# Silu on ScalarE in place of tanh and a VectorE product in one layer of a four-layer graph kernel, and table loads in its instruction planner

## The chip, the cores and the metric

The kernel runs on one core of a Trainium2 chip. Five engines of the core matter here. TensorE (PE in the profile) does matrix products and transposes into the eight banks of PSUM. VectorE (DVE) and ScalarE (ACT) do elementwise work; ScalarE also evaluates functions such as Tanh, Exp, Ln and Silu, which it reads from a table that a separate instruction loads. GpSimd (POOL) does a few small powers and one addition per group. SyncE (SP) issues most transfers. Each engine works through its own queue in order, and engines wait for each other by semaphores.

The metric is device time in microseconds (us) of one execution, as the median of several runs. All data are float32.

## What is computed

The input is 128 graphs with 64 nodes and 256 features, a 0/1 adjacency matrix for each and a node mask. Four layers follow each other; each adds its result to its input and normalizes the rows.

```
def _L0_gnn_ref(...):                      # gated graph layer, 5 steps
    A = (adj != 0).astype(x.dtype)
    for l in range(5):
        m = jnp.einsum('bnd,de->bne', h, weight[l])
        agg = jnp.einsum('bij,bid->bjd', A, m)
        h = _gru_cell(agg, h, w_ih, w_hh, b_ih, b_hh)   # 2 sigmoids, 1 tanh
    return h * mask[..., None]

def _L1_gnn_ref(...):
    agg = epsilon * x + einsum('bnm,bmd->bnd', adjacency, x)
    h = einsum('bnd,dh->bnh', agg, W1) + b1             # 256 -> 1024
    h = jax.nn.silu(h * rsqrt(mean(h*h) + eps) * rms_weight)
    return einsum('bnh,hd->bnd', h, W2) + b2            # 1024 -> 256

# layer 2: artanh of the row norm, product with adj, tanh of the row norm, projection
# layer 3: attention with exp(e_i + f_j), masked by adj

x = _layernorm(x + _L0_gnn_ref(...)); x = _layernorm(x + _L1_gnn_ref(...))
x = _layernorm(x + _L2_gnn_ref(...)); x = _layernorm(x + _L3_gnn_ref(...))
```

## The kernel before, in words

**Tiling.** Eight graphs form a group: four blocks of 128 rows, two graphs in each block. There are 16 groups (0 to 15). `group(g)` records all four layers of a group. Layer 0 (`gated`, called five times) works on features by rows (`hT`), in two halves of 256 rows; its products are `p_r`, `p_in`, `p_hn`, `p_u`, `p_v`, `p_w` (L663), its tanh instructions stand at L767 and L780, and its new state `hT` is formed by three VectorE instructions at L782, L786 and L788. `ps_hr` (L643) are transposes of the state, `ps_agg` (L333) products with the adjacency.

**The order of the work is planned.** Nothing is issued while `group` runs. Each call of `flow.op` records an operation with its engine, a cost in us written by hand (`act`, `dve`, `pe`, `pool` give it from the width), and what it reads and writes; `flow.either` records one that ScalarE or VectorE may take (`copied` L349 and L350, `scaled` L354 and L355). At the end `flow.issue` runs a beam search: `Plan.advance` picks, again and again, the operation that can start first by these costs, out of up to four groups at once (`WINDOW`) and within a look-ahead on each engine (`AHEAD`). The plan found is written into the program as the order of every engine's queue. So a change of a cost, or of one operation, can move any instruction of the program, and which of ScalarE and VectorE takes an `either`.

**Tables.** Before this change the planner knows nothing of table loads. The Ln of layer 2 (L975) is written down as if it were 2600 elements wide, which makes its cost 2.27 us, and the first Tanh (L466) costs 1.5 us. The loads themselves are put in when the program is built, ahead of an activation whose function is not in the table at hand. Tanh (L767, L780, L1012) and Exp (L1045) share one table, Ln needs another.

**Layer 1 of a group**, the place of the change:
- The rows after the first normalization (`x_n`) are multiplied with the adjacency into `ps_agg` and copied to `aggm`. POOL adds the bias b2 to `x_n` in one instruction of 128x1024 (`xb`, L853).
- The hidden layer has 1024 features in eight chunks of 128x512 (`hid`). Groups 0 to 13 form it with seven products in place of eight (`by_sums`, matmuls at L882, differences `t` at L878, sums at L887); groups 14 and 15, the last two, form it plainly (`as_it_is`, `ps_hid`, one copy per chunk).
- For each chunk ScalarE squares it (L868) and VectorE adds the squares (`sqs`, L870). TensorE sums over the features (`ps_ss`), VectorE scales (`ms`, L931), POOL takes the power -1/2 (`rms`, L933), TensorE spreads the result over the partitions (`ps_rms`, L936).
- For each chunk: VectorE adds the bias and multiplies with `ps_rms` (L941); ScalarE takes Tanh of it with the scale `half_r`, half the RMS weight (L944), into a buffer `th`; VectorE forms (th + 1) times the chunk (L946). With v the normalized chunk and w the RMS weight, this is 2 v sigmoid(w v).
- TensorE multiplies with W2 (`ps_o`, 32 calls of `matmul`, which the trace shows as 64 matmuls). The RMS weight that belongs in front of v was multiplied into W2 once, at the start (`w2s`, L590, eight instructions on ScalarE). VectorE takes half of the product and adds `xb` (L959).

Behind it stand the second normalization (statistics L673 and L674, `ve` L676, POOL's power L678, L680, `off` L684, `x_n` L354 or L355), layer 2 (`fac` with Ln at L975, `tan`, `ps_sup`, a row norm at L1006 and L1010, tanh at L1012, `y` at L1028) and layer 3 (`ps_T`, `ps_a`, Exp at L1045, `ps_att`, `y` at L1061).

## Time and profile before

| | |
|---|---|
| Five runs, us | 2431.09, 2433.07, 2432.07, 2430.45, 2430.65; median 2431.09 |
| The profiled execution, us | 2431.09 |
| Span of its profile, us | 2429.3 |
| Granted TensorE clock, mean | 0.996 |
| Read from and written to HBM, MB | 25.74 and 8.39 |

The profile is of one execution. Its span runs from the first instruction to the last one; the execution's own time is 1.8 us longer. PE is TensorE's matmuls, PEld its weight loads, which overlap them. Matmuls are pipelined, so one matmul of 128x256 is shown with about 379 ns while the next starts 216 ns after it; a busy TensorE may still hide short gaps. Idle time of an engine that is not the bottleneck costs nothing.

### The profile page before, as it was taken

How to read it: one execution, taken by the hardware profiler on the slowest of the kernel's cores; microseconds unless marked ns; L12 is line 12 of the kernel's file. 1: busy time of each engine (PE TensorE's matmuls, PEld its weight loads, DVE VectorE, ACT ScalarE, POOL GpSimd, SP SyncE). 2: the span in 40 equal slices, each digit the busy share in tenths (PEclk: the TensorE clock that was granted, in tenths of full speed). 3: DMA queues.
4: the chain of work that ended last, by engine and by line, in shares of the span. 5: the costliest groups of instructions: out<-in, count | busy, mean ns of one | idle time of the engine just before them, and what ended most of it. 6: DMA issues, size and time to landing. Idle time of an engine off the chain costs nothing.

```text
span 2429.3 us, 32703 instructions
## 1 busy us (share of the span) xinstructions
PE 2392.2 (98%) x12258; PEld 2101.7 (87%) x12258; DVE 1893.6 (78%) x4097; ACT 1148.3 (47%) x2408; POOL 188.4 (8%) x144
## 2 busy tenths in 40 slices
PE   9999999999999999999999999999999999999995
PEld 7888888888888888888888888888888888888864
DVE  3668787887888877778777887888787787878777
ACT  4434544454445444454444545455444544445453
POOL 4000000000100000000000100000000000000011
PEclk9999999999999999999999999999999999999998
DMA  4000000000000000000000000000000000000000
GB/s 126 4 1 12 1 29 1 18 12 1 29 1 27 3 18 11 1 27 3 11 19 1 29 1 27 3 18 11 1 29 1 18 12 1 27 9 18 9 9 18
DMA packets 39725, 36.21 MB, mean 15 GB/s; under 512 B 9956, under 2 KB 38656, under 8 KB 39568
## 3 DMA queue, kind: packets, MB, share of 16 engines
q1 hardware_dynamic: 37840, 32.25, 4.3%
q8 instruction: 97, 1.59, 0.3%
q10 hardware_dynamic: 1328, 1.31, 0.2%
q0 software_dynamic: 400, 0.57, 0.1%
q14 instruction: 60, 0.49, 0.1%
HBM read 25.74 MB, written 8.39 MB: 14 GB/s over the span
## 4 chain that ended last, share of the span: by engine, by line
PE 94%; DVE 4%; ACT 1%; DMA 1%; issue 0%; POOL 0%; SPq 0%; POOLq 0%; ACTq 0%; DVEq 0%
PE p_v L663 11%; PE p_w L663 11%; PE p_in L663 11%; PE p_r L663 11%; PE p_hn L663 11%; PE ps_o L333 9%; PE ps_agg L333 6%; PE p_u L663 6%; PE ps_hr L643 3%; PE ps_a L333 2%; PE p_wh L882 2%; PE p_vh L882 2%; PE p_1h L882 2%; PE ps_T L633 1%; PE ps_att L333 1%; PE p_uh L882 1%
## 5 line engine op out<-in xcount | busy, mean ns | idle before, releaser
L663 PE MATMUL p_hn<-hT,w_hn 128*128 128x256 f32 x1280 | 322.8, 380 | 0.0
L663 PE MATMUL p_in<-agg,w_in 128*128 128x256 f32 x1280 | 315.3, 379 | 0.0
L663 PEld LDWEIGHTS p_in<-agg,w_in 128*128 128x128 f32 x1280 | 240.2, 190 | 31.1
L663 PEld LDWEIGHTS p_hn<-hT,w_hn 128*128 128x128 f32 x1280 | 227.9, 191 | 22.7
L333 PE MATMUL ps_o<-w2s,hid 128*128 128x256 f32 x1024 | 231.2, 379 | 0.0
L333 PEld LDWEIGHTS ps_o<-w2s,hid 128*128 128x128 f32 x1024 | 193.9, 190 | 27.3 <-issue 1.2
L678 POOL TENSOR_TENSOR rstd<-ve,pow 128x4 f32<-128x4 f32 (+1 forms) x64 | 82.7, 1292 | 1492.0 <-DVE ve L676 1484.1
L767 ACT ACTIVATE V<-V,half_b 128x256 f32<-128x256 f32 x160 | 72.7, 500 | 199.2 <-DVE V L763 199.0
L663 PE MATMUL p_u<-tA,s 128*128 128x256 f32 x640 | 158.1, 381 | 1.4 <-DVE tA L746 0.6
L663 PE MATMUL p_w<-tA,s 128*128 128x256 f32 x640 | 158.1, 379 | 0.0
L663 PE MATMUL p_r<-hT,a 128*128 128x256 f32 x640 | 156.9, 379 | 0.0
L663 PE MATMUL p_r<-agg,a 128*128 128x256 f32 x640 | 156.7, 379 | 0.0
L663 PE MATMUL p_v<-tB,s 128*128 128x256 f32 x640 | 155.4, 379 | 0.0
L663 PE MATMUL p_v<-tB,na 128*128 128x256 f32 x640 | 154.5, 379 | 0.0
L663 PE MATMUL p_w<-hT,s 128*128 128x256 f32 x640 | 154.3, 379 | 0.0
L349 ACT COPY agg<-ps_agg 128x512 f32<-128x512 f32 x154 | 90.0, 585 | 114.0 <-PE ps_agg L333 98.5
L333 PEld LDWEIGHTS ps_agg<-edge,hr 128*128 128x128 f32 x1024 | 136.1, 191 | 6.6
L354 ACT ACTIVATE hnb<-p_hn,half_b 128x256 f32<-128x256 f32 x232 | 101.8, 473 | 81.3 <-PE p_hn L663 67.3
L333 PE MATMUL ps_agg<-edge,hr 128*128 128x128 f32 x1024 | 138.8, 275 | 0.0
L663 PEld LDWEIGHTS p_u<-tA,s 128*128 128x128 f32 x640 | 119.3, 190 | 21.0 <-DVE tA L746 2.3
L663 PEld LDWEIGHTS p_v<-tB,s 128*128 128x128 f32 x640 | 120.9, 190 | 16.3 <-PE ps_att L333 0.2
L663 PEld LDWEIGHTS p_w<-hT,s 128*128 128x128 f32 x640 | 120.7, 190 | 16.0
(233 smaller groups left out, 4682.5 us busy)
## 6 DMA issues: line engine op xcount, KB each, us to landing
x<-in_x_dram SPq DMA_DIRECT2D x16, 512.0 KB, 3.6
xr<-in_x_dram SPq DMA_DIRECT2D x16, 512.0 KB, 3.6
out_dram<-x_n SPq DMA_DIRECT2D x16, 512.0 KB, 2.9
edge<-in_adj_dram SPq DMA_DIRECT2D x32, 64.0 KB, 2.3
wm<-in_L_gnn_weight_dram SPq DMA_DIRECT2D x5, 256.0 KB, 5.3
w2s<-in_L_gnn_W_dram SPq DMA_DIRECT2D x1, 1024.0 KB, 10.2
w<-in_L_gnn_W_dram SPq DMA_DIRECT2D x2, 512.0 KB, 3.5
w_in_L_gnn_w_hh_dram<-in_L_gnn_w_hh_dram ACTq DMA_DIRECT2D x1, 512.0 KB, 5.2
```

Of the source, the lines that this page charges most:

```text
L333: return nc.tensor.matmul(o, lhsT, rhs, start=(k == 0), stop=(k == nk - 1))
L349: flow.either([("ACT", 0.27 + 0.00077 * n, lambda: nc.scalar.copy(o(), i())), ("DVE", 0.16 + 0.00105 * n, lambda: nc.vector.tensor_copy(o( ...
L354: flow.either([("ACT", 0.27 + 0.00077 * n, lambda: nc.scalar.activation(o(), i(), AF.Identity, bias=bias(), scale=scale())), ("DVE", 0.16 ...
L633: turn(lambda j=j, c=c: nc.tensor.transpose(ps[:, c * HR + j * P:c * HR + (j + 1) * P], src[:, 2 * n + j, c * P:(c + 1) * P], ident.tile() ...
L643: turn(lambda j=j, c=c: nc.tensor.transpose(ps[:, j * D + c * P:j * D + (c + 1) * P], src[:, c, (2 * n + j) * P:(2 * n + j + 1) * P], iden ...
L663: pe(256, lambda c=c, k=k: nc.tensor.matmul(ps[:, c * HR:(c + 1) * HR], w[:, k, c * P:(c + 1) * P], v(k), start=first and c == k == 0, sto ...
L678: pool(1.1, lambda: nc.gpsimd.tensor_tensor(rstd[:, :m, :], ve[:, :m, :], pow2[:, :m, :], OP.pow), [rstd], [ve])
L767: act(256, lambda c=c: nc.scalar.activation(o[:, c, :], src(c), AF.Tanh, bias=half_b[:, i * KD + c:i * KD + c + 1], scale=0.5), [(o, c)], ...
L882: pe(256, lambda c=c: nc.tensor.matmul(ps[:, c * HR:(c + 1) * HR], w1f[:, w, (2 * q + c) * P:(2 * q + c + 1) * P], v[0](), start=first and ...
```

## The change

Layer 1's activation becomes one ScalarE instruction per chunk, Silu in place, with the RMS weight as its scale per partition. The VectorE product L946 and the buffer `th` go, and with them the factors that belonged to them: `half_r`, the eight scalings of W2 and the factor 0.5 behind `ps_o`, which becomes a plain add.

```
-            th = u("VZR"[c % 3], f"th{c}")
-            act(512, lambda v=v, th=th, c=c: nc.scalar.activation(th.tile(), v, AF.Tanh, scale=half_r[:, c:c + 1]),
-                [th], [*parts, half_r])
-            dve(512, lambda v=v, th=th: nc.vector.scalar_tensor_tensor(
-                v, th.tile(), 1.0, v, OP.add, OP.mult), parts, [*parts, th])
+            act(512, lambda v=v, c=c: nc.scalar.activation(v, v, AF.Silu, scale=rmsc(c)), parts, [*parts, cols], SILU)
...
-                dve(256, lambda ps=ps, b=b, j=j: nc.vector.scalar_tensor_tensor(
-                    y1[:, b, :], ps[:, j * D:(j + 1) * D], 0.5, xb[:, b, :], OP.mult, OP.add), [(y1, b)], [ps, (xb, b)])
+                dve(256, lambda ps=ps, b=b, j=j: nc.vector.tensor_add(
+                    y1[:, b, :], ps[:, j * D:(j + 1) * D], xb[:, b, :]), [(y1, b)], [ps, (xb, b)])
...
-    dve(4, lambda: nc.vector.tensor_scalar(half_r.tile(), cols[:, 2 * NV + KH:], 0.5, None, OP.mult), [half_r], [cols])
...
-    for k in range(KH):
-        act(256, lambda k=k: nc.scalar.activation(w2s[:, k, :], w2s[:, k, :], AF.Identity, scale=rmsc(k)), [(w2s, k)], [(w2s, k), cols])
```

The planner learns of tables. An activation may carry `sets`, the tables that hold its function, the first being the one that a load would bring. A plan remembers the table at hand; an activation that is not in it is taken to start `TABLE` later. The costs that stood in for loads are taken back: in the planner's account Tanh is in the table of Exp and in that of Silu, Ln is 4 elements wide, and the first Tanh costs 0.2 us.

```
+    TABLE = 1.28
...
                             elif o.kb and e != "POOL":
                                 t = max(t, self.lands[0])
+                        elif o.sets and self.table not in o.sets:
+                            t += flow.TABLE
...
             _, o, eng, t = best
+            if o.sets and self.table not in o.sets:
+                self.table = o.sets[0]
...
+    TANH, EXP, LN, SILU = ("exp", "silu"), ("exp",), ("ln",), ("silu",)
...
-    def act(n, run, w, r):
-        flow.op("ACT", 0.27 + 0.00077 * n, run, w, r)
+    def act(n, run, w, r, sets=None):
+        flow.op("ACT", 0.27 + 0.00077 * n, run, w, r, sets=sets)
...
-    flow.op("ACT", 1.5, lambda: nc.scalar.activation(warm, one4, AF.Tanh))
+    flow.op("ACT", 0.2, lambda: nc.scalar.activation(warm, one4, AF.Tanh), sets=TANH)
...
-        act(2600, lambda: nc.scalar.activation(fac.tile(), fac.tile(), AF.Ln), [fac], [fac])
+        act(4, lambda: nc.scalar.activation(fac.tile(), fac.tile(), AF.Ln), [fac], [fac], LN)
```

The Tanh and Exp instructions of layers 0, 2 and 3 get their `sets` in the same way. Nothing else is computed differently.

## The prediction

> **What bounds the kernel now.** I read four views in this order: the page, a table of stretches, the waits of TensorE, the groups of instructions. The page first.

> ```profile
> span 2429.3 us, 32703 instructions
> ...
> PE 2392.2 (98%) x12258; PEld 2101.7 (87%) x12258; DVE 1893.6 (78%) x4097; ACT 1148.3 (47%) x2408; POOL 188.4 (8%) x144
> ```

> TensorE is busy for all but 37.1 us. The change touches none of its 12258 matmuls, so what it can win is in those 37.1 us, and what it can lose is new idle time there. So the question is where they lie. The table of stretches has one row per stretch: its length, then busy time and instruction count of PE, PEld, DVE, ACT and POOL, then the clock.

> ```profile
> 0.00:40.00 40.00, 36.12 (x181) 27.41 (x182) 16.03 (x45) 14.27 (x33) 9.02 (x16) 1.00 0.56 169
> 40.00:2300.00 2260.00, 2257.12 (x11665) 2000.88 (x11664) 1777.97 (x3775) 1071.11 (x2251) 160.67 (x116) 1.00 0.04 12
> 2300.00:2340.00 40.00, 36.03 (x156) 25.27 (x156) 31.41 (x55) 20.23 (x38) 6.61 (x4) 1.00 0.05 14
> 2340.00:2382.30 42.30, 42.30 (x181) 31.85 (x179) 32.62 (x72) 22.57 (x35) 3.66 (x3) 1.00 0.00 1
> 2382.30:2429.30 47.00, 20.63 (x82) 16.25 (x80) 35.53 (x150) 20.10 (x53) 8.40 (x7) 0.78 0.07 23
> ```

> Idle: 3.9 us in the start, 2.9 us in the 2260 us of the middle, 4.0 us where the last group enters layer 1 (2300 to 2340), none up to the last `ps_o` matmul at 2382.3, and 26.4 us in the 47.0 us behind it, a serial chain of the last two groups. The waits of TensorE in the middle, and then in 2300 to 2340 (who waited for whom: total, times, longest):

> ```profile
> PE p_uh L882 <- DVE t L878: 1.4, 4, 0.6
> PE p_u L663 <- DVE tA L746: 0.6, 1, 0.6
> PE p_u L663 <- ACT junk_a L1006: 0.5, 1, 0.5
> ```

> ```profile
> PE ps_hid L333 <- DVE aggm L350: 2.5, 1, 2.5
> PE ps_hr L643 <- DVE hT L788: 1.4, 1, 1.4
> ```

> VectorE stands behind most of it, ScalarE behind 0.5 us. The groups that the change removes or resembles (line, engine, operation, names, count | busy, mean ns | idle before):

> ```profile
> L944 ACT ACTIVATE th<-hid,half_r 128x512 f32<-128x512 f32 x128 | 88.0, 721 | 47.1 <-DVE hid L941 47.1
> L946 DVE SCALAR_TENSOR_TENSOR hid<-th,hid 128x512 f32<-128x512 f32 x128 | 82.7, 686 | 0.3 <-ACT th L944 0.2
> L959 DVE SCALAR_TENSOR_TENSOR xb<-ps_o,xb 128x256 f32<-128x256 f32 x64 | 24.4, 420 | 55.1 <-PE ps_o L333 55.1
> L975 ACT ACT_TABLE_LOAD x15 | 19.2, 1283 | 0.3
> L767 ACT ACT_TABLE_LOAD x10 | 12.8, 1283 | 0.2
> L590 ACT ACTIVATE w2s<-w2s,cols 128x256 f32<-128x256 f32 x8 | 3.5, 501 | 0.0
> ```

> **The change part by part.** *VectorE loses* 128 instructions of L946, 82.7 us busy: 1893.6 to about 1811. It is not the bound, so this counts only where TensorE waits for it. L959 becomes a plain add of the same shape and stays at about 420 ns. `half_r` at L490 (one instruction of 162 ns at 11.7 us) goes too.

> *ScalarE* does Silu in place of Tanh, 128 times on 128x512. No row shows Silu. The nearest is L944, 721 ns, with the same shape and a scale read per partition; the copy of that shape (585 ns) bounds it below, two passes of L944 (1442 ns) above. I take 721: no change. Eight scalings at L590 go, 3.5 us, all before 52 us; TensorE idles 3.9 us before 40 us, mostly ahead of them, so I count 0, at best -0.8.

> *Table loads.* The trace has 31 (1 at the start, 15 before Ln, 15 back). In the changed program's order ScalarE's queue has 46: 1 at the start, 15 before Silu, 15 before Ln, 15 back to Tanh or Exp. (Groups 14 and 15 share theirs.) That is 15 x 1.283 = 19.2 us more on an engine at 47%: 1148.3 - 3.5 + 19.2 = 1164 us. What waits behind a load is the Silu of that group and then copies (`agg`, `hr`) and tanh of the other groups. They are covered by the matmuls of up to three other groups: the 29 loads of the middle in this trace go with 0.5 us of TensorE waiting for ScalarE, 0.02 us a load. So 15 more cost 0.3 us, at worst 15 x 1.283 = 19.2 with no cover.

> [...]

> *The middle, new order.* The search runs again, so all queues are reordered. Of the 2.9 us idle, 2.0 are waits for VectorE (`t`, `tA`); with 4% less work there I take half of that as gone, -1.0, bounds -2.9 (all idle gone) and +3 (as much again). With the loads: -0.7.

> *The last group enters layer 1, place one.* In 2300 to 2340 VectorE's hT (L786) took 2.73 us in place of 0.69, from 2301.99, while POOL added `xb` from 2301.69 to 2304.17; `ps_hr` waited 1.4 us. In the new order the `ps_hr` of group 15 again follows `ps_agg` of group 14, behind three VectorE instructions (p_w add, two for hT, 0.7 us each). If the last is held in the same way, `ps_hr` starts about 2.5 + 0.5 us after `xb` starts, less 0.4 for the matmuls still running: idle up to 3.1; if all three come first, 0.3. I take 2.2, as the last of three is nearest to the held case: +0.8.

> *Place two.* Here is what the 2.5 us wait was:

> ```profile
> 2333.94 3.44 DVE L870 TENSOR_TENSOR sqs<-sqs,sq 128x512 f32<-128x512 f32 x2
> 2334.17 2.66 POOL L853 TENSOR_TENSOR xb<-x_n,b_r 128x1024 f32<-128x1024 f32 x1 [1.76 <-DVE x_n L355]
> 2337.31 0.68 DVE L350 COPY aggm<-ps_agg 128x512 f32<-128x512 f32 x1
> 2338.13 0.67 PE L333 MATMUL ps_hid<-aggm,w 128*128 128x512 f32 x1 [2.54 <-DVE aggm L350]
> ```

> The second `aggm` copy stood on VectorE behind a held sum of squares. In the new order both copies are ScalarE's, so this wait goes. But all seven sums of squares of group 14 now stand ahead of group 15's `ve` on VectorE (one did before), and TensorE has `ps_ss` of group 14 ahead of group 15's `ps_agg`. From E, the end of group 14's last `ps_hid` matmul: copy 0.59 and Square 0.72 on ScalarE; on VectorE two `y` (0.87) and one statistics (0.42) from E+0.75, then the last sum (0.70), done at E+2.7. `ps_ss` 0.9, to E+3.65. VectorE's three further statistics steps (0.18, 0.39, 0.18) and `ve` to E+3.7; POOL's power 1.40 with hand-overs, E+5.2; `off` and the first `x_n`, so `ps_agg` starts at E+5.95; the second `x_n` on ScalarE is done at 6.55, `ps_agg` at 7.75; copy 0.59; `ps_hid` resumes at E+8.5. TensorE's work in it is 0.44 + 0.9 + 1.78 + 0.44 = 3.56, so 4.9 us idle in place of 2.5: +2.4, bounds 3.5 (`x_n` of the first blocks ready earlier) and 6.0.

> *Behind it* ScalarE has, for 13.8 us of `ps_hid` matmuls, a load 1.28, six Silu 4.1, seven copies 4.1, eight Squares 5.6: 15.1 us. That ends about 1.4 us after them, and 3.0 us of `ps_o` of group 14 cover it; nothing is added unless a Silu takes longer than 721 ns.

> *The end.* The new order lets group 15 lead and ends with 15 calls of group 14's `ps_o`, 30 matmuls of 0.216 us (74 take 15.99 us in the chain of waits), 6.5 us, where 40 stood, 8.6 us. The leader then does not share VectorE with the other's statistics before its `fac`. Followed with these rows, its L680 falls at 2.25 us before the last `ps_o` (2.15 in the trace), the tanh chain waits for POOL's second power and comes at 10.8 us behind it (11.1 in the trace); from there the queues are the same. So -0.3, bounds -2 and +2.

> Sum: 0 - 0.7 + 0.8 + 2.4 - 0.3 = +2.2 us on the span of 2429.3. The profiled execution took 2431.09, which is also the median of the five, so 1.8 us lie around the span; forecast 2433.3.

> **The rivals.** *(1) Relief of VectorE wins.* For it: 4 of the 5 waits shown are for VectorE, which gets 82.7 us lighter. Against it: only 2.9 us are there in the middle. All of them gone and 2300 to 2340 as it was: 2428.2; with its 4.0 us gone as well, 2424.2.

> *(2) The loads show.* One mechanism: the 15 loads before Silu, in the middle, each keep another group's `agg` or `hr` copy waiting while TensorE runs out. It decides from 0.33 us a load (4.9 us in all). At half a load uncovered, 9.6 us: 2440.7; at all, 2450.3. Against it: 0.02 us a load with the 29 there are.

> *(3) The entry of group 15 is dearer.* Place one at 3.1, place two at 6.0, nothing won in the middle: +5.1, 2436.2; each 0.1 us by which Silu exceeds 721 ns adds 0.6 us in the stretch behind it. For it: ScalarE's 15.1 against 13.8 us.

> *(4) The change does not do what it says*, Silu and Tanh from one table with no load back: the order has the loads; no time would move, 2431.1.

> **How the numbers follow.** A measurement of this kernel (five runs from 2430.45 to 2433.07) tells 0.2% from no change, 4.9 us: faster is below 2426.2, slower above 2436.0. My forecast has 0.53, all of it within 0.2%, own range 2428 to 2436. Rival 1 has 0.20, 0.09 of it faster and 0.11 the same; rival 2 0.12 and rival 3 0.13, both slower; rival 4 0.02, the same. So faster 0.09, same 0.66, slower 0.25. The range reaches below to 2427.5, into rival 1, and above to 2440, to where rival 2 has half a load uncovered.

> **What would show it.** PE busy 2392 as now; 46 loads of 1283 ns; no L946 and VectorE near 1811 us; Silu at 721 ns; under 4 us of PE idle between 40 and 2300; a wait of `ps_hr` and waits of `ps_ss` and `ps_agg` in the last group's entry; 47 us from the last `ps_o` to the end. The forecast is wrong if TensorE's waits for ScalarE exceed 5 us in the middle, if Silu takes over 0.9 us, or if the end differs by more than 2 us from 47.

## The result, and the profile after

The changed kernel takes 2437.43 us (median of 30 runs, 2435.43 to 2438.64), the kernel before 2431.93 us in the runs beside it: ratio 1.0022, 95% interval 1.0017 to 1.0027, 5.5 us more. The profiled execution took 2436.26 us, with a span of 2434.4 us, 5.1 us above that of before. The page:

```profile
span 2434.4 us, 32492 instructions
...
PE 2397.0 (98%) x12258; PEld 2106.4 (87%) x12258; DVE 1812.4 (74%) x3955; ACT 1165.3 (48%) x2428; POOL 187.0 (8%) x144
```

VectorE and ScalarE came out as foreseen. TensorE did not: the same 12258 matmuls are busy 4.8 us longer. The work is the same, and the clock column says what made it longer. The table of stretches (length, then busy time and count of PE, PEld, DVE, ACT and POOL, then the clock):

```profile
0.00:40.00 40.00, 37.52 (x189) 29.23 (x190) 16.90 (x46) 14.18 (x33) 10.23 (x17) 1.00 0.53 169
40.00:2300.00 2260.00, 2253.98 (x11649) 1998.63 (x11648) 1711.42 (x3657) 1085.48 (x2267) 160.97 (x116) 1.00 0.04 12
2300.00:2340.00 40.00, 36.51 (x154) 26.28 (x153) 25.73 (x50) 20.03 (x38) 2.17 (x3) 0.98 0.04 14
2340.00:2387.00 47.00, 47.00 (x191) 35.37 (x189) 23.91 (x57) 24.26 (x37) 4.87 (x3) 0.95 0.00 1
2387.00:2434.40 47.40, 22.01 (x82) 16.91 (x80) 34.44 (x147) 21.35 (x56) 8.73 (x7) 0.70 0.07 23
```

The clock of the stretch from 2340 us, fully busy before and after, fell from 1.00 to 0.95. In the middle 6.0 us are idle, of which 2.4 us are place one, which this order has from 2295.8 us on, ahead of the 2300 us line. TensorE's waits from 40 to 2290 us, and then from 2290 to 2345 us:

```profile
PE p_uh L885 <- DVE t L881: 1.1, 3, 0.4
PE ps_hr L646 <- DVE hT L791: 0.8, 1, 0.8
PE p_u L666 <- DVE tA L749: 0.6, 3, 0.3
PE p_r L666 <- ACT U L357: 0.4, 1, 0.4
PE p_wh L885 <- DVE t L881: 0.3, 1, 0.3
```

```profile
PE ps_hr L646 <- DVE hT L791: 2.4, 1, 2.4
PE ps_ss L339 <- DVE sqs L873: 1.9, 1, 1.9
PE ps_agg L339 <- DVE x_n L363: 1.6, 1, 1.6
```

In the middle 0.4 us of waiting are for ScalarE, although 42 of the 46 loads are there, and 2.8 us are for VectorE, which has 81 us less to do (2.0 us before). The second block is places one and two of the prediction. Silu and the loads ahead of it:

```profile
L945 ACT ACTIVATE hid<-hid,cols 128x512 f32<-128x512 f32 x128 | 83.1, 714 | 15.1 <-DVE hid L943 14.9
L945 ACT ACT_TABLE_LOAD x15 | 19.2, 1283 | 0.3
```

Now the clock around place two, in steps of 2 us (length, PE busy, clock), and the matmuls in it (start, us):

```profile
2334.00:2336.00 2.00, 0.71 (x5) 1.00 0.00 0
2336.00:2338.00 2.00, 1.05 (x8) 1.00 0.00 0
2338.00:2340.00 2.00, 0.74 (x3) 0.52 0.00 0
2340.00:2342.00 2.00, 2.00 (x12) 0.50 0.00 0
2342.00:2344.00 2.00, 2.00 (x10) 0.50 0.00 0
2344.00:2346.00 2.00, 2.00 (x4) 0.77 0.00 0
```

```profile
2336.60 1.05 PE L339 MATMUL ps_ss<-ones,sqs 128*128 128x1 f32 x8 [1.89 <-DVE sqs L873]
2339.26 3.75 PE L339 MATMUL ps_agg<-edge,x_n 128*128 128x128 f32 x16 [1.60 <-DVE x_n L363]
```

TensorE is mostly idle from 2334.7 to 2339.3 us, and the granted clock is 0.50 for the 6.8 us from 2338.1. The 16 `ps_agg` matmuls take 3.75 us; 16 of the same kind took 1.95 us at place one.

Following starts of matmuls against their steady spacing, the 5.1 us between the two profiles are: start -1.3, middle +1.2 (0.7 of it idle time), place one +1.0, place two with the half clock +3.65, end +0.56 (47.55 us behind the last `ps_o` start, where 47.0 stood).

### The profile page after: what moved, and what is told of

Its sections match the earlier page's. It is cut to its first block, busy times and chain, and to the rows that moved or that the text cites. A ratio compares the mean times of both kernels' runs of the same rounds, so it can differ in the third digit from the quotient of the medians.

```text
span 2434.4 us, 32492 instructions
## 1 busy us (share of the span) xinstructions
PE 2397.0 (98%) x12258; PEld 2106.4 (87%) x12258; DVE 1812.4 (74%) x3955; ACT 1165.3 (48%) x2428; POOL 187.0 (8%) x144
## 3 DMA queue, kind: packets, MB, share of 16 engines
q10 hardware_dynamic: 1328, 1.31, 0.2%
## 4 chain that ended last, share of the span: by engine, by line
PE 86%; DVE 4%; POOL 1%; ACT 1%; issue 0%; POOLq 0%; ACTq 0%; DVEq 0%
PE p_v L666 10%; PE p_w L666 10%; PE p_in L666 10%; PE p_r L666 9%; PE p_hn L666 9%; PE ps_o L339 9%; PE ps_agg L339 6%; PE p_u L666 5%; PE ps_hr L646 2%; PE ps_a L339 2%; PE p_wh L885 2%; PE p_vh L885 2%; PE p_1h L885 2%; PE ps_sup L339 1%; PE ps_hid L339 1%; PE ps_att L339 1%
## 5 line engine op out<-in xcount | busy, mean ns | idle before, releaser
L339 PE MATMUL ps_o<-w2s,hid 128*128 128x256 f32 x1024 | 224.9, 379 | 0.0
L666 PEld LDWEIGHTS p_v<-tB,na 128*128 128x128 f32 x640 | 120.5, 190 | 16.0 <-DVE V L766 0.2
```

What stands on the lines that cost most here:

```text
L339: return nc.tensor.matmul(o, lhsT, rhs, start=(k == 0), stop=(k == nk - 1))
L666: pe(256, lambda c=c, k=k: nc.tensor.matmul(ps[:, c * HR:(c + 1) * HR], w[:, k, c * P:(c + 1) * P], v(k), start=first and c == k == 0, sto ...
```

## The experiments

Each kernel was timed beside the kernel before, whose median was 2431.88 to 2431.97 us in the series. Where nothing else is said, a kernel is the changed one with the edit shown.

**Are the loads the cost?** `no_silu_load` keeps every queue's order and takes the 15 loads ahead of Silu away. The activation then lacks the product with its argument.

```
-            act(512, lambda v=v, c=c: nc.scalar.activation(v, v, AF.Silu, scale=rmsc(c)), parts, [*parts, cols], SILU)
+            act(512, lambda v=v, c=c: nc.scalar.activation(v, v, AF.Tanh, scale=rmsc(c)), parts, [*parts, cols], SILU)
```

> The changed kernel with the very same order in every queue, but Silu is issued as Tanh, which shares the table of the gates: 31 table loads in place of 46, 19.2 us less on ScalarE. It leaves out the product with the argument in layer 1's activation. Theory A (the 5.5 us were lost where the last group enters layer 1, and none of it to the loads): 2436.5 to 2437.5 us, TensorE waits as in the changed kernel. Rival B (the loads show on TensorE): a quarter of the 19.2 us alone would bring it to 2432.5 us or below.

Measured: 2436.63 us, ratio 1.0021 (1.0012 to 1.0030). ScalarE has 31 loads, TensorE's waits in the middle are the same to 0.3 us, and `ps_ss` and `ps_agg` wait 1.9 and 1.6 us as before. The time is where theory A expected it: in this order the loads are hidden, and the loss stays without them.

**Is it the clock?** `fill_entry` leaves the order and gives TensorE something to do in the two waits of place two.

```
+    def busy(ps, n, i):
+        return [nc.tensor.transpose(ps[:, (k % 4) * P:(k % 4 + 1) * P], ident.tile(), ident.tile()) for k in range(n)] + [i()]
...
-            pe(1, lambda ps=ps, b=b: matmul(ps[:, b:b + 1], sqs[:, b * P:(b + 1) * P], ones, 0, 1), [ps], [sqs])
+            pe(1, lambda ps=ps, b=b: busy(ps, 14 if g == 14 and not b else 0, lambda: matmul(
+                ps[:, b:b + 1], sqs[:, b * P:(b + 1) * P], ones, 0, 1)), [ps], [sqs])
...
+                    pe(128, lambda j=j, c=c: busy(ps, 12 if g == 15 and top and not (n or j or c) else 0, lambda: matmul(
```

> The changed kernel's order, with 14 transposes of the identity issued ahead of ps_ss of group 14 and 12 ahead of ps_agg of group 15, into columns that the real matmuls then write: TensorE is busy in the 1.9 and 1.6 us in which it waited, and the waits themselves are as long as before. Theory A (3 of the 5.5 us are TensorE at half clock behind these two waits): the granted clock stays at 1.00 from 2334 to 2346 us, the 16 ps_agg take about 1.95 us in place of 3.75, ps_rms 0.44 in place of 0.85, the first two ps_hid 0.86 in place of 1.72, and the time falls by about 3.0 us, to 2434.4. Rival (the clock there sets nothing, since the waits and the engines behind them set the end): 2437 us, no change.

Measured: 2434.37 us, ratio 1.0010 (1.0001 to 1.0019), 3.1 us below the changed kernel, as theory A expected. The clock and the matmuls in its trace:

```profile
2338.00:2340.00 2.00, 1.87 (x17) 1.00 0.00 0
2340.00:2342.00 2.00, 1.79 (x17) 1.00 0.00 0
```

```profile
2337.66 1.51 PE L345 MATMUL ps_agg<-ident 128*128 128x128 f32 x12
2339.31 2.05 PE L339 MATMUL ps_agg<-edge,x_n 128*128 128x128 f32 x16
```

`ps_agg` starts at the same moment (2339.31 for 2339.26): its input came no earlier. It takes 2.05 us in place of 3.75. So idle time that nobody could use was made harmless by useless work; about 3 of the 5.5 us were the clock.

**Place one.** `xb_dve` issues the `xb` of group 14 on VectorE, at a point where that engine was idle (it is kept back until the later of two `hT` updates of group 15 is issued).

```
+    HELD = [({("xb", 14)}, ("st", 15, 3, 1))]
...
+            if o.tag == ("xb", 14):
+                eng, o.ways = "DVE", {"DVE": o.ways["POOL"]}
```

> The changed kernel with the xb of group 14 taken off GpSimd and issued on VectorE behind the hT that ends at 2302.6 us, where VectorE was idle for 5.4 us (1.25 us of work by its width). Theory A (hT L791 at place one takes 2.72 us only because xb runs beside it on GpSimd): hT takes 0.69 us, the wait of ps_hr falls from 2.44 to about 0.4 us, the time falls by 2.0 us to 2435.4. Rival (hT is long for another reason, or the 2 us are lost again at place two): 2437 us.

Measured: 2432.93 us, ratio 1.0007 (0.9998 to 1.0016). The same `hT` instruction in the changed kernel, with GpSimd's `xb` beside it, and then in `xb_dve`:

```profile
2295.03 2.53 POOL L856 TENSOR_TENSOR xb<-x_n,b_r 128x1024 f32<-128x1024 f32 x1 [2.83 <-ACT x_n L362]
2295.39 2.72 DVE L791 SCALAR_TENSOR_TENSOR hT<-hT,R 128x512 f32<-128x512 f32 x1
```

```profile
2295.98 0.69 DVE L817 SCALAR_TENSOR_TENSOR hT<-hT,R 128x512 f32<-128x512 f32 x1
```

`hT` is short again and the wait of `ps_hr` fell from 2.44 to 0.41 us. The median fell by 4.5 us where the trace explains 2.0 and theory A expected 2.0; the interval holds both. The profiled execution, 2434.91 us, is the slowest of the eleven and lies 1.35 us below the changed kernel's profiled one. A likely reason for the larger step of the medians stands in the last section: in the trace of `no_silu_load` the same wait of 2.44 us has a clock of 0.50 for 3.41 us behind it.

**The order of place two.** `entry_order` moves five pieces of the order (each set is kept back, with all that depends on it, until the named operation is issued):

```
+    HELD = [({("hid", 14, 5), ("hid", 14, 6), ("hid", 14, 7)}, ("hr", 15, 1)),
+            ({("sqs", 14, 4), ("sqs", 14, 5), ("sq", 14, 6)}, ("ve n0", 15)),
+            ({("sqs", 14, 6), ("sqs", 14, 7), ("sq", 14, 7)}, ("x n0", 15)),
+            ({("ss", 14)}, ("hid", 15, 0)),
+            ({("rms out", 14)}, ("hid", 15, 2))]
```

> The changed kernel with five moves in the order at the last group's entry, and nothing else changed: the last ps_hr of group 15 goes three chunks of ps_hid up, the last sums of squares of group 14 go behind group 15's ve, ps_ss of 14 behind group 15's ps_agg and first ps_hid, ps_rms of 14 two chunks later. Theory A (place two and the clock behind it are the loss): both waits of 1.9 and 1.6 us go, a wait of about 0.8 us for the aggm copy comes, ps_agg runs at full clock; 4 to 6 us less, 2431.5 to 2433.5. Rival C (the loss is spread over the replanned middle and the end): at most 1 us less, 2436.5 or above.

Measured: 2434.98 us, ratio 1.0016 (1.0007 to 1.0024): 2.5 us gained, less than either end of the expectation for theory A. TensorE's waits from 2330 to 2365 us:

```profile
PE ps_o L360 <- ACT hid L990: 1.4, 2, 1.1
PE ps_hid L360 <- ACT aggm L378: 0.7, 1, 0.7
PE ps_agg L360 <- DVE x_n L384: 0.6, 1, 0.6
PE ps_agg L360 <- ACT x_n L383: 0.5, 1, 0.5
PE ps_ss L360 <- DVE sqs L909: 0.3, 1, 0.3
```

They add up to 3.5 us, as 1.9 + 1.6 did: waiting was moved about, not removed. But it now lies in five pieces, and the clock stays at 1.00 from 2330 to 2380 us. What was gained is the clock. The largest piece is new: `ps_o` waits for Silu, which I had put too late.

**The end chain.** `fill_end` puts transposes ahead of `ps_sup` (14 for group 15, 44 for group 14) and ahead of the first `ps_T` (34), with the function of `fill_entry`.

> The changed kernel's order with transposes of the identity in the three longest TensorE waits of the end chain: 14 ahead of ps_sup of group 15, 44 ahead of ps_sup of group 14, 34 ahead of the first ps_T. Theory A (half clock behind a wait lengthens the chain that ends the kernel): ps_sup takes 1.97 us twice in place of 3.66 and 3.75, the first ps_T 1.03 in place of 1.97, ps_a of group 15 3.75 in place of 4.47; 3 to 5.2 us less, 2432.3 to 2434.5 us. Rival (the end chain is set by VectorE, ScalarE and GpSimd, TensorE's part is beside it): 2436.5 us or above.

Measured: 2435.24 us, ratio 1.0014 (1.0005 to 1.0023), 2.2 us gained, less than the 3 to 5.2 us of theory A. In its trace:

```profile
2389.67 1.99 PE L339 MATMUL ps_sup<-tan,adjT 128*128 128x256 f32 x8 [0.36 <-DVE tan L995]
2397.52 1.99 PE L339 MATMUL ps_sup<-tan,adjT 128*128 128x256 f32 x8 [1.05 <-DVE tan L995]
2404.96 1.15 PE L639 MATMUL ps_T<-ident,x_n 128*128 128x128 f32 x8 [1.74 <-ACT x_n L365]
2406.29 5.44 PE L339 MATMUL ps_a<-wattT,x3T 128*128 128x258 f32 x16 [0.18 <-ACT x3T L360]
```

Both `ps_sup` are at full clock (3.66 and 3.75 us without the filling), but the 1.74 us left ahead of `ps_T` brought half clock (0.50) 1.9 us later, under `ps_a`, and the other engines set part of this chain.

**Half of the change at a time.** `plan_only` has the planner's account and the old activation (Tanh, `half_r`, `th`, the VectorE op, scaled W2); `silu_only` has Silu and the old planner (no `sets`, Ln 2600 wide).

> The planner's account of table loads alone; the activation is as before (Tanh, and the VectorE op that finishes it, so VectorE has its 82.7 us back; 31 table loads). Its order at the last entry has ps_agg of group 15 ahead of ps_ss of group 14, and only three sums of squares ahead of group 15's ve. Theory A (the loss is the order that the search happened on for the last group's entry): no pair of waits there, clock 1.00 over the 16 ps_agg, 2429 to 2432.5 us. Rival D (the account itself makes the plan worse, whatever the activation): 2436 us or more.

Measured: 2443.57 us (five runs, 2439.35 to 2444.07), ratio 1.0042 (1.0029 to 1.0055). A clear miss for theory A, and what rival D expected; against rival D speaks `after_stretch` below, which has the same account. I had read the order at the entry and thought it good; TensorE's waits from 2290 us on say why not (the trace is of an execution of 2440.33 us, 3.2 below the median):

```profile
PE ps_sup L339 <- DVE th L1024: 6.7, 1, 6.7
PE ps_T L640 <- ACT x_n L362: 4.6, 1, 4.6
PE ps_agg L339 <- ACT x_n L362: 3.3, 1, 3.3
PE ps_ss L339 <- DVE sqs L877: 2.1, 1, 2.1
PE ps_o L339 <- DVE hid L952: 2.0, 2, 1.4
```

The first two belong to the end chain and are of like size in the changed kernel (5.4 and 4.6 us). `ps_agg` stands first but waits 3.3 us for `x_n`, half clock follows for 3.4 us, from 2338.84 to 2342.25, and `ps_ss` of group 15 and `ps_o` find VectorE late, which still has the product to do. In 40 to 2290 us 5.0 us are idle as well, where the kernel before has 2.9.

> Silu in place of Tanh and the VectorE op, without the account: the planner costs every activation as before, so 49 table loads lie where it knows nothing of them. In its order group 14 runs far ahead of group 15, and more loads stand in the end chain. Theory A (loads and Silu cost nothing while TensorE has work; only the entry and the end count): TensorE waits for ScalarE in the middle below 1.5 us in all; the time by entry and end alone, 2431 to 2437 us. Rival B (loads that the plan does not know of show): 18 loads more than before at 1.28 us, of which a half uncovered, 2443 us or more.

Measured: 2436.60 us, ratio 1.0021 (1.0012 to 1.0030). It has 49 loads. In 40 to 2290 us TensorE waits 3.4 us for ScalarE, 3.0 of them for Silu ahead of `ps_o`, more than the 1.5 us that theory A allowed and far less than rival B's half. The time is inside theory A's range. Not one pair of waits but another stands among the last two groups (`ps_rms` 1.3 us, `ps_o` 1.6 us), with half clock for 6.8 us from 2371.2; what each part costs is not shown.

**Other orders of the same work.** The search is given another setting, and nothing else is changed: the first added line in `after_wide`, the second in `after_stretch` and, on the kernel before, in `before_stretch`.

```
-    WINDOW, STRETCH, WIDTH, LAG = 4, 25.0, 8, 40.0
+    WINDOW, STRETCH, WIDTH, LAG = 4, 25.0, 12, 40.0
+    WINDOW, STRETCH, WIDTH, LAG = 4, 20.0, 8, 40.0
```

> The changed kernel with a search that keeps 12 plans in place of 8 and so finds another order from group 4 on. Theory A (the change costs nothing of its own; its 5.5 us are the one order that this search found): the time moves by several us either way, anywhere from 2429 to 2441 us, with the difference from the changed kernel again in TensorE's waits and clock behind 2290 us, and in 40 to 2290 us the waits for ScalarE stay below 1.5 us. Rival D (Silu with its 15 loads, or the account, costs 4 to 6 us whatever the order): 2436 to 2438 us.

> The changed kernel with plans compared every 20 us in place of every 25: a third order of the same work. Theory A: as for after_wide, 2429 to 2441 us, and not the same as it. Rival D: 2436 to 2438 us.

> The kernel before with plans compared every 20 us in place of every 25: another order of the same work, with Tanh and the VectorE op. Theory A (the order found sets some us either way, in the kernel before too, whose own order was a good one): 2433 to 2442 us. Rival D (orders differ by less than a us or two, and the change's 5.5 us are its own): 2430 to 2433 us.

Measured: `after_wide` 2443.17 us, ratio 1.0046 (1.0034 to 1.0059); `after_stretch` 2431.48 us, ratio 1.0001 (0.9992 to 1.0010); `before_stretch` 2431.59 us, ratio 1.0000 (0.9991 to 1.0008). The changed kernel, with the same Silu and the same account, lies 11 us above the kernel before in one order (15 loads ahead of Silu) and level with it in another (16 of them, 49 loads in all): rival D falls. Theory A has the sign but not the size: `after_wide` is above its 2441 us, and the waits for ScalarE in the middle are 2.0 us where it allowed 1.5. The expectation for `before_stretch` was a miss, its other order is as good as its own. TensorE's waits of `after_wide` from 2290 us:

```profile
PE ps_sup L339 <- DVE th L1016: 6.7, 1, 6.7
PE ps_T L636 <- ACT x_n L362: 5.4, 2, 4.6
PE ps_o L339 <- ACT hid L945: 2.7, 1, 2.7
PE ps_hid L339 <- DVE aggm L358: 2.5, 1, 2.5
```

Here `ps_o` of the last groups does wait for Silu, and in its middle 6.9 us are idle where the changed kernel has 3.6 (40 to 2290 us); 2.0 us there are for ScalarE's copies. In `after_stretch` 1.3 us are idle in the middle. Its last two groups are not free of waits (`ps_o` 2.3 us for Silu, `ps_ss` 2.2 us, half clock twice for 3.4 us), but its end chain is short: 42.2 us from the start of the last `ps_o` matmul to the end, where the changed kernel has 47.6, `after_wide` 49.7, the kernel before 47.0 and `before_stretch` 46.4. So an order sets the time in three places: the middle, the entry of the last group, and the end. And in `before_stretch`, a kernel without Silu, this stands at the entry:

```profile
2332.89 1.49 PE L333 MATMUL ps_ss<-ones,sqs 128*128 128x1 f32 x8 [2.10 <-DVE sqs L870]
2336.00 3.76 PE L333 MATMUL ps_agg<-edge,x_n 128*128 128x128 f32 x16 [1.63 <-DVE x_n L355]
```

It is place two of the changed kernel, pair of waits and half clock and all (mean clock 0.93 from 2290 to 2340 us). That loss comes from an order which either kernel can be given, not from Silu; `before_stretch` has it and is level all the same.

**All repairs together.** `all_four` joins `xb_dve`, `entry_order` (with `ps_ss` directly behind `ps_agg` and `ps_rms` one chunk earlier) and `fill_end`. `best` then differs from it in three places:

```
-            ({("ss", 14)}, ("agg", 15, 1)),
+            ({("ss", 14)}, ("hid", 15, 0)),
...
-                pe(256, lambda b=b, j=j, ps=sup[h]: busy(ps, {14: 44, 15: 14}.get(g, 0) if not b else 0, lambda: matmul(
+                pe(256, lambda b=b, j=j, ps=sup[h]: busy(ps, {14: 52, 15: 16}.get(g, 0) if not b else 0, lambda: matmul(
...
-            feats_of(x3T, x3, n, {14: 0, 15: 34}.get(g, 0))
+            feats_of(x3T, x3, n, {14: 0, 15: 48}.get(g, 0))
```

> The changed kernel with xb of group 14 on VectorE, the order of the last entry moved as in entry_order but with ps_ss of group 14 directly behind group 15's ps_agg and ps_rms one chunk earlier, and the transposes of the end chain. Theory A (the pieces are independent): 2.0 us for place one, 2.5 us for the entry as entry_order measured and 1.5 more for the Silu waits of 1.4 us that it ran into, 3 to 5 us for the end: 2426.5 to 2429 us, below before. Rival (one loss takes the place of another): above 2431.9 us.

Measured: 2431.57 us, ratio 0.9999 (0.9990 to 1.0008). 5.9 us gained, 3 to 5 less than the sum: `ps_ss` directly behind `ps_agg` waits 1.87 us for the last sum of squares, and the end is no shorter than in `fill_end` (46.0 us behind the last `ps_o` start in both, 47.6 in the changed kernel).

> As all_four, with ps_ss of group 14 behind the first chunk of group 15's ps_hid (all_four had TensorE wait 1.87 us for it directly behind ps_agg), and 16, 52 and 48 transposes in the end chain, where 0.36, 1.05 and 1.73 us of wait were left and the last of them brought the clock to 0.50 under ps_a. Theory A: 1.2 us less at the entry, 0.5 to 1 us less in the end, 2429.3 to 2430.3 us, below before. Rival (another wait takes its place): 2431.5 us or above.

Measured: 2428.79 us, ratio 0.9989 (0.9980 to 0.9998), 8.6 us below the changed kernel and 3.2 below the kernel before, a little better than theory A expected. In its trace:

```profile
2399.81 1.15 PE L662 MATMUL ps_T<-ident,x_n 128*128 128x128 f32 x8 [0.20 <-ACT x_n L388]
2401.14 3.75 PE L362 MATMUL ps_a<-wattT,x3T 128*128 128x258 f32 x16 [0.18 <-ACT x3T L383]
```

`ps_a` is at 3.75 us where `fill_end` has 5.44. The kernel before was not given the same repairs, so nothing is said of which of the two would win with them.

## Why the prediction was right, and where it was not

The forecast was 2433.3 us with a range of 2427.5 to 2440; 2437.43 us lies inside, 0.22% above before, at the border between no change and slower. There is luck in that. The prediction called 2428 to 2436 its own range and put the stretch up to 2440 there for rival 2, the loads, which is not what happened; the most likely class by its chances was "the same" (0.66, slower 0.25). One of its signs failed outright: TensorE was to be busy for 2392 us as now, and was busy for 2397. By its steps:

- **TensorE is the bound, VectorE's 82.7 us win nothing.** Right. VectorE went to 1812.4 us (1811 foreseen), and its waits in the middle did not shrink: 2.8 us for 2.0. The -1.0 us taken for relief there was wrong in sign; the middle came to +1.2 us, not -0.7. Rival 1 falls with it, and rival 4 by the 46 loads.
- **Silu at 721 ns.** It is 714.
- **Table loads.** 46 loads at 1283 ns, ScalarE at 1165.3 us (1164 foreseen), 0.4 us of TensorE waiting for ScalarE in the middle. `no_silu_load` tells the price of the 15: 0.8 us between the medians, inside the intervals; 0.3 was foreseen. Rival 2 falls, for this order. `silu_only` and `after_wide` show that other orders do pay: 3.0 us of waiting for Silu in the middle in one, 2.7 us at its end in the other. With a load between two activations, the second starts 1.31 us behind the end of the first, in the median of the 46 and in that of the 31 before; 1.28 us of it are the load.
- **Place one**, +0.8 with `ps_hr` idle for 2.2: +1.0, idle 2.4. Right, and so was the cause: `hT` takes 2.72 us beside GpSimd's `xb` and 0.69 us without it. The upper bound is added up wrongly: 2.5 + 0.5 - 0.4 is 2.6, not the 3.1 that rival 3 uses too; the 2.2 does not rest on it.
- **Place two**, +2.4: this term was mis-sized, and it holds most of the error. Order, waits and their releasers were as foreseen. Idle time was 3.5 us, less than the 4.9 us worked out; but the step counted TensorE's work in it at full speed ("0.44 + 0.9 + 1.78 + 0.44 = 3.56"), and behind the two waits the clock was 0.50 for 6.8 us. The term came to +3.65: about 1.0 of longer waiting (3.5 us for 2.5) and 2.7 of clock, which `fill_entry` puts at 3.1. So two errors cancel in part, idle time put too high and the clock put at nothing. The prediction's own table had the warning, a clock of 0.78 in the 47 us of the end chain. No rival had it: rival 3 gave 2436.2 us, close to what was measured, but by 6.0 us of idle time that was not there.
- **Behind it.** Nothing was added in the changed kernel: from 2340 us to the last `ps_o` TensorE is busy throughout. The margin is not large, though: `entry_order` left 9.0 us between `ps_rms` of group 14 and the first `ps_o`, where the changed kernel has 15.3, and `ps_o` waited 1.4 us for Silu.
- **The end**, -0.3: +0.56. The first `ps_sup` of the end chain ran at half clock (3.66 us; 1.97 before), which may have taken back what the leader's head start was to give; which links of the chain it lengthened is not shown.
- **The start**, 0: -1.3; TensorE is idle for 2.5 us there, not 3.9. Not foreseen, and not followed up.

The longest wait does not tell how long the half clock lasts: it is 1.9 us at place two, with 6.8 us of half clock behind it, 3.3 us in `plan_only` and 1.7 us in `fill_end`, with 3.4 us in each.

What stays open: whether the account makes bad orders likelier. Of four orders found with it, three are slow (2437.4, 2443.2, 2443.6 us) and one is not (2431.5); of three without it, one is slow (2436.6; the others 2431.9 and 2431.6). Sorted by the activation the count is the same: of four with Silu three are slow, of three with Tanh one. That is too few to say.

## What to carry to other kernels

Where a planner or scheduler orders the work, a change of one operation draws a new order, and the luck of that draw (12 us here, between two orders of one kernel) can be larger than the change: measure more than one order before judging the change. On a kernel with a busy TensorE, price a wait as its length plus what the clock takes behind it; two short waits close together can cost nearly as much again as they last (3.5 us of waiting and 3.1 us of clock here). Where such a wait can't be removed, idle TensorE time can be filled with work that nobody reads (26 transposes in `fill_entry`, 3.1 us less).

## What the hardware showed that I had not expected

```profile
2293.72:2297.13 3.41, 2.09 (x18) 1.88 (x16) 3.18 (x4) 2.98 (x7) 2.10 (x1) 1.00 0.30 107
2297.13:2300.54 3.41, 2.29 (x15) 2.16 (x16) 2.34 (x4) 1.47 (x3) 0.43 (x1) 1.00 0.00 0
```

```profile
2295.47:2298.88 3.41, 0.97 (x10) 0.81 (x9) 3.38 (x3) 1.50 (x4) 2.36 (x1) 1.00 0.00 0
2298.88:2302.29 3.41, 3.41 (x13) 2.87 (x12) 2.22 (x5) 1.39 (x3) 0.00 (x0) 0.50 0.01 2
```

```profile
2333.42:2336.84 3.42, 2.17 (x17) 1.75 (x15) 3.31 (x4) 2.26 (x4) 2.66 (x1) 1.00 0.00 0
2336.84:2340.25 3.41, 2.12 (x5) 1.06 (x6) 2.44 (x4) 0.85 (x2) 0.00 (x0) 1.00 0.00 0
```

- Where the wait was split over two windows (2.09 and 2.29 us busy, 2.17 and 2.12 us), the clock stayed at 1.00; where it lay in one (0.97 us busy), the next window was at 0.50. In `after_wide` a wait of 2.53 us lies in one window (0.88 us busy) and half clock follows for 3.41 us; in the changed kernel the waits of 1.9 and 1.6 us leave 1.08 us busy in the window up to 2338.09. In all 14 traces cut this way, from the first record of the clock on (6.79 us in the changed kernel), a window at full clock in which TensorE was busy for less than 1.4 us was always followed by half clock, one with more than 1.8 us never, and full clock came back only behind a window busy for 2.9 us or more. Between 1.4 and 1.8 us both are found: 1.46 and 1.72 us with full clock behind them in the kernel before, 1.53 us with half clock in the changed one. (The ends of matmuls are modelled, so these bounds are rough.) One order can so lose some 1.7 us at place one (an estimate, half of 3.41), as in `no_silu_load`, or nothing, as in the changed kernel, by where the windows happen to lie.
- Transposes of the identity kept the clock up here: with them TensorE is busy for 3.04 us in the window of `fill_entry` up to 2338.66 us, and the clock stays at 1.00.
- The scatter of the runs seems to belong to the clock too (likely, not shown: one execution of each kernel has a trace). Eleven runs of `best` lie within 0.6 us (2428.50 to 2429.08); those of the changed kernel within 3.2 us, of `all_four` within 3.1 us and of the kernel before within 2.3 us in that series (27 runs). `best` and `all_four` differ in one position and 24 transposes, and in the trace of `best` the clock stays at 1.00 up to 2417 us. Of the changed kernel's executions, those from 2438.08 us up have a mean clock of 0.992 and those below 2436 us one of 0.994 or 0.995. In the kernel before the mean clock does not sort them (0.994 at 2430.3 and at 2432.6 us alike).
